# Earlier adjacency transposes, early TensorE work and later row sums in a two-layer graph network

## The chip, the cores and the metric

The kernel runs on one core of one Trainium2 chip. The metric is device time in microseconds for one launch, and lower is better. The core has five engines that run side by side, each working through its own list of instructions in order: TensorE (PE, matrix multiplication), VectorE (DVE), ScalarE (ACT), GpSimd (POOL) and SyncE (SP), which here issues nearly all transfers between device memory and on-chip memory. An engine waits only where an instruction names a semaphore that another engine or a transfer has yet to raise.

## What is computed

The input x has 16 batches of 1024 nodes with 256 channels; the adjacency is one 1024 x 1024 matrix for all batches. There are two layers, each closed by a layer norm without scale and offset. Cut to what matters:

```python
# layer 0, for each batch
c = mean(x over channels)                      # one number a node
A = 1 - |tanh((c_m - c_n) / 2)|                # likeness of two nodes, symmetric
g = relu((x.T @ (adj * A)) * para)             # the query graph: 256 x 1024
q = g as 4 heads of 64;  k, v = x @ kv_w       # keys and values
x = layernorm(x + softmax(q k.T / 8) v)
# layer 1
h = relu(x w1_loop + adj (x w1_neigh) + b1)    # 128 wide
h = relu(h w2_loop + adj (h w2_neigh) + b2)    # 256 wide
x = layernorm(x + (x + h) / 2)
```

Layer 0 needs the rows of adj as they lie (x.T times adj); layer 1 needs adj transposed. Everything is float32.

## The kernel before

**Stages.** The order of all work is written out by hand in `run()`; inside its `manual_schedule` block nothing is rearranged. For batch 0 the kernel makes keys (line 350) and values (362) from x, and then the query graph of batch 0: eight steps `q.step(t)` (line 400), each with one 128-row tile of the weighted adjacency `wg`. ScalarE makes the likeness (lines 386 and 387), VectorE multiplies it with adj (392). `q.end()` (lines 406 and 407) turns the sums into the queries qT. Then come 16 rounds, one a batch. Round b holds the attention of batch b in four units (`scores`: matmuls at 516, exponentials at 519, running sum of them on VectorE at 523 and 525; `outputs`: matmuls at 536), the first graph convolution of batch b-1 and the second of batch b-2 between the units, and after the last unit the query graph, keys and values of batch b+1. So each round ends in a transition, and it is there that the change works.

**Two kinds of query graph.** Batches 0 and 1 use `Queries`, with eight plain steps. Batches 2 to 15 use `FastQueries`, which builds the product from seven smaller products p[1] to p[7] in four steps (line 473). Its `end()` adds them up on VectorE: ScalarE copies p[1] to P1 (line 482), the first addition makes U (483), and five more lines (484 to 489) make the rest of U and qT. The seven products lie in PSUM: p[1] and p[6] in one tile of two banks, p[7] and p[5] in a second, p[2] and p[3] in a third, p[4] in a single bank. There are three such two-bank tiles in all, and the keys of the next batch take the first and then the second of them. The first half of the keys can therefore start when line 483 has read p[1] and p[6], and the second half when line 488 has read p[5].

**The norm.** The layer norm of layer 0 (`BlockedNorm`) runs during the same transition, on x in blocked form: `mean()` subtracts the mean of each row (lines 309 and 312, VectorE), `squares()` squares on ScalarE (318), sums the squares on VectorE (319) and joins the two halves (260), `variance()` folds the sums with a small matmul (256) between the two halves of the keys, `scale()` and `spread()` follow after the keys. For batches 1 to 14 `norm.mean()` and `norm.squares()` are called in the middle of the third step of the query graph, and `q.end()` comes one step later.

**The transposed adjacency.** It is made once. `adj_blocked(mt)` (line 207) loads 128 columns of adj with four transfers of 128 KB, in pieces of 128 bytes, so that a 32 x 32 transpose on VectorE (`turn_adj`, line 871) gives the full transpose: 16 instructions for eight tiles. Three quarters of the result stay in fixed tiles, the fourth in two tiles (rows01). In the kernel before, the loads are issued among the steps of the query graph of batch 1, and the 16 transposes come behind `norm.spread()` in the same transition. The first reader is the graph convolution of batch 0 in round 1 (line 654).

**Buffers and queues.** All 128 x 1024 working tiles come from one pool of 23 (`row_tile`). A transfer needs a free tile, and its completion is counted on one of eight counters in turn, so that SP holds a transfer back until the eighth one before it has landed. VectorE does what stands in its list in order: an instruction that waits for a transfer holds up everything behind it.

**The start.** x of batch 0 comes in four pieces (line 117). TensorE's first work is to transpose it (line 227), as each piece lands.

Of the kernel before, what the change touches and what calls it, by code (L numbers as in the profile page):

```python
# [12 lines left out]
AF = mybir.ActivationFunctionType  # L13
# [5 lines left out]
def kernel(  # L19
# [281 lines left out]
    class BlockedNorm:  # L301
# [10 lines left out]
                nc.vector.tensor_sub(x_cc, x_cc, mean.unsqueeze(2).to_broadcast([P, NB, S]))  # L312

        def squares(self):
            self.part = small.tile([P, NC, NB], F32, tag="part", name=f"sq_part_{self.name}", bufs=2)
            for cc in range(NC):
                sq = row_tile(f"sq_{self.name}_{cc}")
                nc.scalar.activation(sq, self.xB[cc], AF.Square)  # L318
                nc.vector.tensor_reduce(self.part[:, cc, :], by_node(sq), AX.X, ALU.add)  # L319
            join(self.part)  # L320

        def variance(self):
# [87 lines left out]
    class FastQueries(Queries):  # L410
# [61 lines left out]
                x_n, w_n = terms[n]  # L472
                nc.tensor.matmul(self.p[n], x_n[:, k, :], w_n, start=(k == 0), stop=(k == TJ - 1))  # L473

        def end(self):
            qT = work.tile([P, NC, N], F32, tag="qT", name=f"qT_{self.b}")
            u = row_tile(f"U_{self.b}")
            h0, h1 = ts(0, FB), ts(1, FB)
            p = self.p
            add = nc.vector.tensor_add  # L480
            p1 = row_tile(f"P1_{self.b}")[:, h0]
            nc.scalar.copy(p1, p[1])
            add(u[:, h0], p1, p[6])  # L483
            add(qT[:, 0, h0], p1, p[2])
            add(u[:, h1], u[:, h0], p[7])
            add(qT[:, 1, h0], u[:, h1], p[4])
            add(qT[:, 1, h1], u[:, h1], p[5])
            add(u[:, h0], u[:, h0], p[5])
            add(qT[:, 0, h1], u[:, h0], p[3])
            for cb in range(NC):  # L490
                nc.vector.tensor_mul(qT[:, cb, :], qT[:, cb, :], para_sb[:, cb, :])
                nc.scalar.activation(qT[:, cb, :], qT[:, cb, :], AF.Relu, scale=QSCALE)
            return qT
# [340 lines left out]
    def run():  # L834
# [3 lines left out]

        xT, c_col = prepare_first(x_first)
        q = Queries(0, x_first)
        for t in range(NT):
# [29 lines left out]
        for t in range(NT):  # L873
            if t + 3 < NT:
                q.weigh(t + 3)
            q.step(t)
            if t == 4:
                xB = load_blocked(0, "a0")
                ready = {}
                ready["xT"], ready["part"] = prepare(blocked, "1")  # L880
            if t == 6:
                ready["mean"] = means(ready["part"], "1")
        qT = q.end()
        convs = {}
        for b in range(B):
            more = b + 1 < B
            att = Attention(b, xB, qT, kT, v)
            c1, c2, c3 = (convs.get(b - k) for k in (1, 2, 3))
            both = Joined(c1, c2) if c2 else None
            if c1 and more:  # L890
                xb = load_x(b + 1, str(b + 1))
            if c2 and more:
                c2.load_h1()

            def gap0():
                blocked = load_blocked(b + 1, str(b + 1))
                c1.inner()
                att.add(0)
                if both:
                    c2.load_x()  # L900
                    both.fetch(2, 3)
                    both.left(nc.gpsimd)
                ready["xT"], ready["part"] = prepare(blocked, str(b + 1))

            def weigh_first():
                q.times_adj(0)
                q.times_adj(TJ)
                q.right(0)

            def next_means():  # L910
                q.c_row, q.c_col = means(ready["part"], str(b + 1))

            def gap1():
                for t in (0, TJ):
                    q.load(t)
                if both:
                    both.fetch(1, 4)
                    both.run({1: (lambda: q.left(nc.gpsimd),),
                              2: (lambda: att.add(1), next_means),
                              6: (lambda: q.likeness(0), lambda: c3 and c3.moments()),  # L920
                              7: (lambda: q.likeness(TJ),),
                              5: (weigh_first,),
                              4: (lambda: c3 and c3.finish(out[b - 3]),),
                              3: (c1.turn_blocks,)})
                else:
                    q.left(nc.gpsimd)
                    next_means()
                    att.add(1)
                    for t in (0, TJ):
                        q.likeness(t)  # L930
                    store("01", rows01)
                    adj_sums(rows01)
                    weigh_first()
                    c1.first(rows01)
                    c1.turn_blocks()

            def gap2():
                if both:
                    c2.last()
                att.add(2)  # L940

            between = [gap0, gap1, gap2] if c1 and more else []
            if more:
                q = (FastQueries if c1 else Queries)(b + 1, xb)
            for u in range(len(UNITS)):
                att.scores(u)
                if u == 3 and between:
                    for t in (2, TJ + 2, 3, TJ + 3):
                        q.load(t)
                    for t in (2, TJ + 2, 3, TJ + 3):  # L950
                        q.likeness(t)
                    q.right(1)
                if u and not between:
                    att.add(u - 1)
                att.outputs(u)
                if u == 2 and more:
                    if c1:
                        for t in (1, TJ + 1):
                            q.load(t)
                            q.likeness(t)  # L960
                            q.times_adj(t)
                    else:
                        q.c_row, q.c_col = ready["mean"]
                        for t in range(3):
                            q.load(t)
                            q.weigh(t)
                if u < 3 and between:
                    between[u]()
            norm = BlockedNorm(xB, att.sums, str(b))
            if more and not c1:  # L970
                xT = ready["xT"]
                for t in range(3, NT):
                    q.load(t)
                for t in range(3, NT):
                    q.likeness(t)
                for mt in range(4):
                    tiles[mt] = adj_blocked(mt)
                q.times_adj(3)
                q.step(0)
                q.times_adj(4)  # L980
                q.step(1)
                att.add(3)
                for mt in range(4, NT):
                    tiles[mt] = adj_blocked(mt)
                q.times_adj(5)
                q.step(2)
                q.step(3)
                norm.mean()
                q.times_adj(6)
                q.times_adj(7)  # L990
                q.step(4)
                norm.squares()
                q.step(5)
                q.step(6)
                norm.variance()
                xB = load_blocked(b + 1, f"a{b + 1}")
                q.step(7)
                qT = q.end()
                norm.scale()
                norm.spread()  # L1000
                turn_adj(range(NT))
                kT, v = keys(b + 1, xT), values(b + 1, xT)
            elif more:
                xT = ready["xT"]
                q.pair(2)
                q.step(0)
                q.step(1, lambda: att.add(3))
                q.pair(3)
                q.step(2, lambda: (norm.mean(), norm.squares()))
                q.step(3)  # L1010
                qT = q.end()
                xB = load_blocked(b + 1, f"a{b + 1}")
                kT = keys(b + 1, xT, norm.variance)
                norm.scale()
                norm.spread()
                v = values(b + 1, xT)
            else:
                c2.load_h1()
                c2.load_x()
                both.fetch(2, 3)  # L1020
                c1.inner()
                both.left(nc.gpsimd)
                both.fetch(1, 4)
                both.run({1: (lambda: att.add(3),), 2: (norm.mean, norm.squares), 7: (norm.variance,),
                          5: (norm.scale, norm.spread)})
                c1.turn(0)
                c2.last()
                c1.turn(1)
            convs[b] = GraphConv(b, norm.x1T, norm.nodes)
# [84 lines left out]
```

## Time and profile before

| | us |
|---|---|
| median of 3 runs | 2201.18 (2199.86 to 2201.87) |
| the profiled execution, its own time | 2200.6 |
| its span, first to last instruction | 2198.8 |
| TensorE busy | 2172.8 (99%) |
| VectorE busy | 1864.0 (85%) |
| ScalarE busy | 969.3 (44%) |
| mean granted TensorE clock | 0.997 |

The numbers in the first column of a timeline are microseconds from the start of the span. A group of instructions on one engine that follow each other is one row: its start, the time that it covers, engine, line, operation, the tiles written and read, shapes, and how many. In brackets stand the idle time of the engine just before and what ended it. PEld rows are weight loads of TensorE and run beside its matmuls. A float32 matmul of 512 columns is recorded as two passes, with starts 0.43 us apart when nothing is in the way. Ends of matmuls are modelled, so gaps are best read from starts. A line number is that of the kernel before; in the changed kernel lines from 318 on stand a few lines lower.

### The profile page before, as it was taken

How to read it: one execution, taken by the hardware profiler on the slowest of the kernel's cores; microseconds unless marked ns; L12 is line 12 of the kernel's file. 1: busy time of each engine (PE TensorE's matmuls, PEld its weight loads, DVE VectorE, ACT ScalarE, POOL GpSimd, SP SyncE). 2: the span in 40 equal slices, each digit the busy share in tenths (PEclk: the TensorE clock that was granted, in tenths of full speed). 3: DMA queues.
4: the chain of work that ended last, by engine and by line, in shares of the span. 5: the costliest groups of instructions: out<-in, count | busy, mean ns of one | idle time of the engine just before them, and what ended most of it. 6: DMA issues, size and time to landing. Idle time of an engine off the chain costs nothing.

```text
span 2198.8 us, 22720 instructions
## 1 busy us (share of the span) xinstructions
PE 2172.8 (99%) x8096; PEld 1032.4 (47%) x8096; DVE 1864.0 (85%) x2453; ACT 969.3 (44%) x1064; POOL 328.1 (15%) x177
## 2 busy tenths in 40 slices
PE   8998999999999999999999999999999999999997
PEld 4344444544444444444444445445454444544354
DVE  4988888888898988988889788998989889888965
ACT  4734445434454443545444454434544445434511
POOL 1000020210302103021030301203012020210021
PEclk9999999999999999999999999999999999999999
DMA  8294372633646335463453734527264272733342
GB/s 193 86 139 148 60 182 68 124 125 63 177 100 151 104 58 172 96 172 88 75 162 78 182 86 78 172 58 182 86 92 157 58 182 88 137 114 64 116 134 97
DMA packets 586359, 258.59 MB, mean 118 GB/s; under 512 B 488064, under 2 KB 552448, under 8 KB 586240
## 3 DMA queue, kind: packets, MB, share of 16 engines
q1 hardware_dynamic: 585968, 256.56, 48.4%
q8 instruction: 65, 1.06, 0.2%
q14 instruction: 54, 0.44, 0.1%
q10 hardware_dynamic: 272, 0.52, 0.1%
HBM read 210.90 MB, written 46.14 MB: 117 GB/s over the span
## 4 chain that ended last, share of the span: by engine, by line
PE 72%; DVE 24%; issue 2%; ACT 1%; DMA 0%; DVEq 0%; SPq 0%; POOLq 0%; ACTq 0%; POOL 0%
PE hu_ps L793 16%; PE s L516 15%; PE av L536 15%; DVE acc L525 6%; PE k_ps L350 5%; PE v_ps L362 5%; PE t_ps L634 3%; PE h_ps L700 2%; PE hu_ps L641 2%; PE g_ps L400 2%; PE h_ps L701 2%; DVE wg L392 2%; DVE sq_part L319 1%; DVE wg L446 1%; DVE T L445 1%
## 5 line engine op out<-in xcount | busy, mean ns | idle before, releaser
L519 ACT ACTIVATE pr<-s 128x1024 f32<-128x1024 f32 x512 | 476.1, 1052 | 179.5 <-PE s L516 179.1
L525 DVE TENSOR_TENSOR acc<-acc,pr 128x1024 f32<-128x1024 f32 x384 | 493.2, 1285 | 41.4 <-DVE acc L525 0.9
L516 PE MATMUL s<-qT,kT 64*128 64x512 f32 x2048 | 457.2, 596 | 0.7 <-ACT qT L407 0.7
L536 PE MATMUL av<-pr,v 128*64 128x512 f32 x2048 | 453.6, 595 | 0.0
L516 PEld LDWEIGHTS s<-qT,kT 64*128 64x128 f32 x2048 | 190.9, 186 | 236.5 <-ACT pr L519 114.8
L536 PEld LDWEIGHTS av<-pr,v 128*64 128x64 f32 x2048 | 141.4, 137 | 300.0 <-issue 289.7
L326 POOL TENSOR_TENSOR rstd<-rstd,neg_half 128x32 f32<-128x32 f32 x16 | 87.1, 5441 | 1149.9 <-DVE rstd L324 1149.9
L386 ACT ACTIVATE wg<-c_row,c_col 128x1024 f32<-128x1024 f32 x128 | 147.1, 1149 | 86.5 <-DVE accB L527 50.6
L392 DVE SCALAR_TENSOR_TENSOR wg<-wg,adj 128x1024 f32<-128x1024 f32 x128 | 149.9, 1211 | 10.4 <-ACT wg L387 10.4
L793 PE MATMUL hu_ps<-adj,R 128*128 128x512 f32 x360 | 158.3, 596 | 0.0
L387 ACT ACTIVATE wg<-wg 128x1024 f32<-128x1024 f32 x128 | 135.4, 1058 | 4.1
L350 PE MATMUL k_ps<-xT,kvw_sb 128*128 128x512 f32 x256 | 117.9, 605 | 2.9 <-DVE U L483 2.8
L318 ACT ACTIVATE sq<-xB_a 128x1024 f32<-128x1024 f32 x32 | 33.8, 1057 | 192.4 <-DVE xB_a L312 178.8
L473 PE MATMUL g_ps<-wg,S 128*128 128x512 f32 x224 | 116.7, 603 | 0.0
L473 PE MATMUL g_ps<-T,S 128*128 128x512 f32 x224 | 114.4, 592 | 0.0
L362 PE MATMUL v_ps<-kvw_sb,xT 128*128 128x256 f32 x512 | 113.1, 379 | 0.0
L331 DVE TENSOR_TENSOR xB_a<-xB_a,rstd 128x1024 f32<-128x1024 f32 x32 | 38.8, 1255 | 84.4 <-POOL rstd L326 84.4
L473 PE MATMUL g_ps<-wg,x 128*128 128x512 f32 x224 | 109.0, 599 | 0.0
L362 PEld LDWEIGHTS v_ps<-kvw_sb,xT 128*128 128x128 f32 x512 | 97.3, 190 | 20.1 <-issue 7.7
L523 DVE TENSOR_TENSOR acc<-pr,pr 128x1024 f32<-128x1024 f32 x64 | 78.1, 1220 | 33.8 <-ACT pr L519 33.8
L793 PE MATMUL hu_ps<-adjT,t 128*128 128x512 f32 x240 | 105.7, 592 | 0.0
L793 PEld LDWEIGHTS hu_ps<-adj,R 128*128 128x128 f32 x360 | 67.3, 190 | 78.9 <-issue 75.8
(167 smaller groups left out, 2718.7 us busy)
## 6 DMA issues: line engine op xcount, KB each, us to landing
adj<-in_adj_dram SPq DMA_DIRECT2D x128, 512.0 KB, 4.5
adj<-adjT SPq DMA_DIRECT2D x120, 512.0 KB, 7.5
xB_a<-in_x_dram SPq DMA_DIRECT2D x128, 128.0 KB, 4.1
x1d<-xB_a SPq DMA_DIRECT2D x128, 128.0 KB, 3.4
x<-x1d SPq DMA_DIRECT2D x16, 1024.0 KB, 6.8
xB<-in_x_dram SPq DMA_DIRECT2D x120, 128.0 KB, 4.6
x<-in_x_dram SPq DMA_DIRECT2D x15, 1024.0 KB, 7.0
out_dram<-x SPq DMA_DIRECT2D x15, 1024.0 KB, 4.6
```

Source lines behind the costliest of these rows:

```text
L326: nc.gpsimd.tensor_tensor(self.rstd, self.rstd, neg_half, ALU.pow)
L350: nc.tensor.matmul(pk[:, ts(j, FB)], kvw_sb[:, cc, ts(kb, P)], xT[:, cc, ts(j, FB)], start=(cc == 0), stop=(cc == NC - 1))
L362: nc.tensor.matmul(pv[:, ts(i, C)], xT[:, cc, ts(g * per + i, P)], kvw_sb[:, cc, C:2 * C], start=(cc == 0), stop=(cc == NC - 1))
L386: nc.scalar.activation(wg, self.c_row, AF.Abs, bias=self.c_col[:, t:t + 1], scale=-1.0)
L387: nc.scalar.activation(wg, wg, AF.Tanh, scale=-0.5)
L392: nc.vector.scalar_tensor_tensor(wg, wg, 1.0, self.adj.pop(t), op0=ALU.add, op1=ALU.mult)
L473: nc.tensor.matmul(self.p[n], x_n[:, k, :], w_n, start=(k == 0), stop=(k == TJ - 1))
L516: nc.tensor.matmul(ps[:, ts(s, FB)], self.kT[rows, pair, ts(mt, P)], self.qT[rows, pair, ts(j, FB)], start=True, stop=True)
L519: nc.scalar.activation(pr, ps, AF.Exp)
L525: nc.vector.tensor_add(acc, acc, pr)
L536: nc.tensor.matmul(pav[s * HD:(s + 1) * HD, :], self.v[:, mt, pair * P + s * HD:pair * P + (s + 1) * HD], self.pr[mt][:, ts(s, FB)], start ...
L793: nc.tensor.matmul(dst, self.x[n][:, k, :], half_adj[w][:, k, :] if w else of_rows(rows, k), start=(start and k == 0), stop=(k == TJ - 1), ...
```

## The change

There are three parts.

1. Sixteen transposes of the identity into an unused PSUM bank are put ahead of all other work of TensorE.
2. The eight loads of columns of adj are issued in the query graph of batch 0: tiles 0 to 3 after step 2, tiles 4 to 7 after step 4, the latter ahead of the load of x for the residual of batch 0 (xB). The transposes of tiles 0 to 4 stand behind `prepare` of batch 1 in VectorE's list, ahead of `means` and `q.end()`; those of tiles 5 to 7 stand behind `q.end()`. The old places are empty.
3. `squares()` is cut in two: it keeps the squares on ScalarE, and the new `sum_squares()` has the sums on VectorE. In batches 1 to 14 (14 transitions) the sums are handed to `q.end()`, which calls them just behind its first addition. In batches 0 and 15 both parts are called one after the other, as before.

```diff
         def squares(self):
+            self.sq = [row_tile(f"sq_{self.name}_{cc}") for cc in range(NC)]
+            for cc in range(NC):
+                nc.scalar.activation(self.sq[cc], self.xB[cc], AF.Square)
+
+        def sum_squares(self):
             self.part = small.tile([P, NC, NB], F32, tag="part", name=f"sq_part_{self.name}", bufs=2)
             for cc in range(NC):
-                sq = row_tile(f"sq_{self.name}_{cc}")
-                nc.scalar.activation(sq, self.xB[cc], AF.Square)
-                nc.vector.tensor_reduce(self.part[:, cc, :], by_node(sq), AX.X, ALU.add)
+                nc.vector.tensor_reduce(self.part[:, cc, :], by_node(self.sq[cc]), AX.X, ALU.add)
             join(self.part)
...
-        def end(self):
+        def end(self, between):
...
             add(u[:, h0], p1, p[6])
+            between()
             add(qT[:, 0, h0], p1, p[2])
...
+        idle = bank_psum("idle")
+        for _ in range(16):
+            nc.tensor.transpose(idle[:, 0:P], ident, ident)
         xT, c_col = prepare_first(x_first)
...
             q.step(t)
+            if t in (2, 4):
+                for mt in range(2 * t - 4, 2 * t):
+                    tiles[mt] = adj_blocked(mt)
             if t == 4:
                 xB = load_blocked(0, "a0")
                 ready = {}
                 ready["xT"], ready["part"] = prepare(blocked, "1")
+                turn_adj(range(5))
             if t == 6:
                 ready["mean"] = means(ready["part"], "1")
         qT = q.end()
+        turn_adj(range(5, NT))
...
-                for mt in range(4):
-                    tiles[mt] = adj_blocked(mt)
...
-                for mt in range(4, NT):
-                    tiles[mt] = adj_blocked(mt)
...
-                turn_adj(range(NT))
                 kT, v = keys(b + 1, xT), values(b + 1, xT)
...
                 q.step(2, lambda: (norm.mean(), norm.squares()))
                 q.step(3)
-                qT = q.end()
+                qT = q.end(norm.sum_squares)
```

More of the change, by code (lines that the diff above doesn't have):

```diff
@@ L992, in run @@
                 norm.squares()
+                norm.sum_squares()
                 q.step(5)
@@ L1023, in run @@
                 both.fetch(1, 4)
-                both.run({1: (lambda: att.add(3),), 2: (norm.mean, norm.squares), 7: (norm.variance,),
+                both.run({1: (lambda: att.add(3),), 2: (norm.mean, norm.squares, norm.sum_squares), 7: (norm.variance,),
                           5: (norm.scale, norm.spread)})
```

## The prediction

> **What bounds the kernel now.** I read first the list of TensorE's own waits: engine and line, what ended the wait, microseconds in total, how often, the longest.
>
> ```profile
> PE den_ps L548 <- DVE o L540: 5.6, 1, 5.6
> PE xT_ps L227 <- DMA x<-in_x_dram: 4.9, 2, 4.7
> PE k_ps L350 <- DVE U L483: 2.8, 13, 0.5
> PE den_ps L548 <- DVE den_part L529: 0.8, 1, 0.8
> PE s L516 <- ACT qT L407: 0.7, 1, 0.7
> ```
>
> With one more row of 0.7 this is all: 15.5 us of 2198.8. TensorE is the bound nearly everywhere, so the most that a change outside TensorE can win is some 15 us, while any new wait of TensorE costs its full length. The three parts of the change aim at three of these rows: the second (start), the first (one gap of round 1) and the third (14 transitions).
>
> Next the timeline of one transition, of 14 that look alike:
>
> ```profile
> 393.15 2.36 DVE L312 TENSOR_TENSOR xB_a<-xB_a,mean 128x1024 f32<-128x1024 f32 x2
> 395.56 2.35 DVE L319 TENSOR_REDUCE sq_part<-sq 128x32 f32<-128x1024 f32 x2
> 396.57 0.57 ACT L482 COPY P<-g_ps 128x512 f32<-128x512 f32 x1
> 398.06 0.68 DVE L483 TENSOR_TENSOR U<-P,g_ps 128x512 f32<-128x512 f32 x1
> 398.79 3.70 PE L350 MATMUL k_ps<-xT,kvw_sb 128*128 128x512 f32 x8 [0.17 <-DVE U L483]
> 401.18 0.68 DVE L488 TENSOR_TENSOR U<-U,g_ps 128x512 f32<-128x512 f32 x1
> 402.33 0.30 PE L256 MATMUL sum_ps<-sq_part,fold 128*128 128x32 f32 x2
> 402.47 1.96 PE L350 MATMUL k_ps<-xT,kvw_sb 128*128 128x512 f32 x4
> ```
>
> The sums (L319) stand ahead of U, and the keys' first half starts when U ends. The second half (402.47) needs L488 done; that ended at 401.86, so here it is hidden by 0.6 us.
>
> Then the end of the query graph of batch 0:
>
> ```profile
> 39.02 0.19 DVE L260 TENSOR_TENSOR part<-part 128x32 f32<-128x32 f32 x1
> 48.32 0.19 DVE L265 TENSOR_SCALAR mean<-mean_ps 128x32 f32<-128x32 f32 x1 [9.11 <-PE mean_ps L256]
> 50.12 1.23 DVE L406 TENSOR_TENSOR qT<-g_ps,para_sb 128x1024 f32<-128x1024 f32 x1
> 56.01 1.22 DVE L523 TENSOR_TENSOR acc<-pr,pr 128x1024 f32<-128x1024 f32 x1 [2.95 <-ACT pr L519]
> ```
>
> VectorE is idle for 9.1 us and again for 3.0 us: this is the room into which the transposes are moved. TensorE's scores start at 52.49, on L406 and the ScalarE step behind it. Last, the transposes' old place and what follows:
>
> ```profile
> 145.45 9.57 DVE L871 STREAM_TRANSPOSE adjT<-adjB 128x512 f32<-128x512 f32 x16
> 155.37 1.22 DVE L523 TENSOR_TENSOR acc<-pr,pr 128x1024 f32<-128x1024 f32 x1 [0.36 <-ACT pr L519]
> 170.33 0.52 DVE L552 RECIPROCAL rden<-den_ps 64x16 f32<-64x16 f32 x2 [2.60 <-PE den_ps L548]
> 190.28 0.64 PE L548 MATMUL den_ps<-den_part,fold 128*128 128x32 f32 x2 [5.56 <-DVE o L540]
> ```
>
> and the rate of the loads (issues by SP; then a window with its GB/s at the end):
>
> ```profile
> 115.55 22.81 SPq L207 DMA_DIRECT2D adjB<-in_adj_dram  x25
> 116.00:138.00 22.00, 22.00 (x57) 10.03 (x56) 17.35 (x25) 2.11 (x2) 2.61 (x1) 1.00 1.31 144
> ```
>
> 25 loads of 128 KB in 22.81 us, 144 GB/s: 0.91 us each.
>
> **What the Trainium skill says.** The page "TensorE: Matmul & The Clock Gate", section "HAM oscillation — how this bites in real kernels", says that an idle TensorE of over about 3.4 us falls to half clock. The trace agrees: behind the 5.6 us gap at 190.28 the window from 190 to 192 us shows a clock of 0.50, and the four matmul passes there are 0.86 us apart instead of 0.43. The same page's Part 4 says that transposes don't count as work in this; here 16 transposes from 4.73 us are followed by key passes that still start 0.86 us apart, which fits but doesn't prove it. "DMA: Bandwidth & Descriptors", section "Why small descriptors are slow (HBM only)", gives a fixed cost per descriptor; the 144 GB/s with 128-byte pieces against 325 GB/s in the window from 10 to 24 us agree in kind.
>
> **The change part by part.** *Transposes leave their old place.* 9.57 us of VectorE go. What is late next? L523 at 155.37 starts on ScalarE's exponential, after 0.36 us of idle, so it can't start earlier; and VectorE is idle again for 2.60 us at 170.33, waiting for TensorE. So no debt of the transposes reaches the gap at 190.28: that debt begins at 170.33, with four 1.2 us instructions of prepare (L216, L249) between. Gain 0 (bounds 0 to 8.7: the 5.6 gap, 2.0 of half clock behind it, 0.8 of the next wait). The loads that leave SP's queue there free it for loads that were on time: 0.
>
> *Loads in the new place.* The first eight take the slots in which xB's eight went before: issued from 28.50, the last at 39.1, landed 3.8 later, at 42.9. Transfers 9 to 20 (through tile 4) follow at 0.91: 42.9 + 12 x 0.91 = 53.8; tile 7 lands at 42.9 + 24 x 0.91 = 64.7. Bounds for the spacing: 0.64 (206 GB/s, window 29 to 36 us, with long rows in it) to 1.17 (112 GB/s, 37 to 43 us). xB is now behind all 32 and lands at 64.7 + 8 x 0.91 = 72.0; its first reader is the first `att.add` at 83.1: hidden by 11 us. Behind it on SP stands the first row tile of batch 1, issued at 66.96 before, needed at 100.1: hidden. The three tiles beyond the 23 take places of adj rows long used: 0.
>
> *Transposes in the new place.* 0.60 us each (9.57/16). Those of tile 4 wait for 53.8, and VectorE's list is held: behind them stand L265, c_row, and L406, on which the scores wait. They end at 53.8 + 1.2 = 55.0. L265 to L406 is 1.80 (50.12 - 48.32), L406 to scores 2.37 (52.49 - 50.12): scores start at 59.2 instead of 52.49, +6.7 (bounds 3.5 to 9.8). TensorE has then been idle for some 8 us, so it starts at half clock: +2.0, as behind 190.28 (four passes at +0.43, and 0.3 around them; bounds 1 to 3.4). The last three tiles end at 64.7 + 1.2 = 65.9; L523 would be due at 56.01 + 6.7 + 2.0 = 64.7. It is 1.2 late, and before the second unit VectorE idles for 1.63 us (at 69.99, on ScalarE): hidden. Without that cover 1.2. Sum of this part: +8.7.
>
> *Transposes of the identity.* 16 x 0.22 us from 1.5 to 5.0 us, 0.3 beyond the first piece of x. If they warm the clock, the half-clock passes (0.7 us) and part of the slow transposes of x go, up to 1.2 us by 12.7 us. But the scores at 59.2 hang on transfers, so this shows as longer idle: 0 (bounds -1.2 to +0.3).
>
> *Sums behind U.* U now needs only the copy P, ended at 397.14, and L312, ended at 395.51: it starts at 397.2, 0.86 earlier, and ends at 397.9. The last graph pass started at 398.03, so the keys start at 398.46, not 398.79: -0.33. The sums then take VectorE for 2.50 us (395.56 to 398.06). The next addition starts at 397.2 + 0.60 + 2.50 = 400.3 instead of 398.66: +1.64. With it L488 ends at 403.5. In the built program the keys' second half waits for just this instruction. TensorE would be there at 398.46 + 3.68 = 402.14 (3.68 from 402.47 - 398.79); it waits 1.4 us and starts at 403.55 instead of 402.47: +1.08. Behind it stand the values and the next scores, with no idle time of TensorE until the next transition, so nothing gives it back. On ScalarE the copies of keys and values come up to 1.64 later; the third group of values needs the first copy at 275.8 in the first transition, and it is there at about 275.5: hidden by 0.3. 14 x 1.08 = +15.1 (bounds 0.9 to 1.3 each: 12.6 to 18.2).
>
> Sum: 2200.6 + 8.7 + 15.1 = 2224.4 for the profiled execution; its time is 0.6 under the median, so 2201.2 + 23.8 = 2225.0.
>
> **The rivals.** *The first graph is free* (B). If tile 4 were there by 48.3, VectorE's idle 9.1 us would hide the ten transposes. That needs 0.45 us a load, half of what the trace shows anywhere for such pieces. Then +15.1 - 1.2: 2215.1.
>
> *The keys' second half doesn't wait* (C). If its tile came free earlier than I read, each transition wins its 0.33: 2201.2 + 8.7 - 14 x 0.33 = 2205.3. Against it: the wait on L488 stands in the program before too.
>
> *VectorE sets the period* (D, not slower). The chain of waits goes through VectorE for 24%, and the steps ahead of U in each transition are its own. If TensorE's even starts hid waiting, a delay of TensorE would be taken up before the next transition, and U's 0.86 would be won: 2201.2 - 14 x 0.86 + 8.7 = 2197.9. The point that decides: TensorE would need over 1.08 us of slack in each round; the list shows 2.8 us in the whole run, at U itself.
>
> **How the numbers follow.** Forecast 0.80, B 0.08, C 0.05, D 0.05, something slower still 0.02. The forecast's bounds are +17 to +31: 2218 to 2232. Reaching to B gives 2213 to 2232. A measurement can tell some 0.2% (4.4 us) from no change: faster 0.02 (D's tail), same 0.06 (half of C, most of D), slower 0.92.
>
> **What would show it.** In the profile after: a wait of TensorE at the keys for the line of L488, 14 times, 1.4 us each; the wait for U gone; the wait of 5.6 us at L548 still there; a VectorE wait for adjB of some 3 us and more ahead of tile 4's transposes; scores of batch 0 at about 59 us with a clock of 0.5. I am wrong if the second half starts within 3.7 us of the first, if the scores start by 53, or if the gap near 190 is gone.

## The result, and the profile after

The changed kernel takes 2228.03 us, the median of 4 runs (2226.10 to 2231.87), against 2201.31 for the kernel before in the same session: 1.0125 times, interval 1.0107 to 1.0142. That is 26.7 us more; the prediction had 23.8 (2225.0, range 2213 to 2232). The profiled execution took 2228.1 us with a span of 2226.2, 27.4 longer than before.

First the list of TensorE's own waits in the changed kernel (engine and line, what ended the wait, us in total, how often, the longest):

```profile
PE k_ps L353 <- DVE U L492: 18.4, 14, 1.6
PE s L520 <- ACT qT L410: 10.0, 1, 10.0
PE den_ps L552 <- DVE o L544: 5.6, 1, 5.6
PE den_ps L552 <- DVE den_part L533: 2.1, 3, 0.8
PE mean_ps L256 <- DVE o L544: 0.9, 4, 0.2
```

L492 is the addition that was L488 before. The wait for U is gone, and 14 waits for L492 of 1.3 us each stand in its place. The start of the scores of batch 0 now costs one wait of 10.0 us. The wait of 5.6 us in round 1, which the earlier transposes were to help, is unchanged. The fourth row has grown from 0.8 and the fifth is new; the prediction had neither. (A row of 1.5 us between them, ahead of the transposes of the identity, is left out here.)

The timeline of the transition that the prediction showed, now in the changed kernel:

```profile
407.23 0.57 ACT L485 COPY P<-g_ps 128x512 f32<-128x512 f32 x1
407.83 0.69 DVE L486 TENSOR_TENSOR U<-P,g_ps 128x512 f32<-128x512 f32 x1 [1.66 <-ACT P L485]
408.44 2.34 DVE L322 TENSOR_REDUCE sq_part<-sq 128x32 f32<-128x1024 f32 x2
409.14 3.60 PE L353 MATMUL k_ps<-xT,kvw_sb 128*128 128x512 f32 x8
413.43 0.68 DVE L492 TENSOR_TENSOR U<-U,g_ps 128x512 f32<-128x512 f32 x1
414.17 3.70 PE L353 MATMUL k_ps<-xT,kvw_sb 128*128 128x512 f32 x8 [1.29 <-DVE U L492]
```

VectorE now idles 1.66 us ahead of U, because the sums no longer fill that time. Then the sums run between U and the rest of the additions. The second half of the keys starts 5.03 us after the first (414.17 - 409.14) instead of 3.68.

And the end of the first query graph, TensorE and VectorE:

```profile
46.87 3.68 PE L403 MATMUL g_ps<-wg,x 128*128 128x512 f32 x8
48.08 1.30 DVE L879 STREAM_TRANSPOSE adjT<-adjB 128x512 f32<-128x512 f32 x2 [2.21 <-DMA adjB<-in_adj_dram]
51.80 1.30 DVE L879 STREAM_TRANSPOSE adjT<-adjB 128x512 f32<-128x512 f32 x2 [2.41 <-DMA adjB<-in_adj_dram]
55.32 1.30 DVE L879 STREAM_TRANSPOSE adjT<-adjB 128x512 f32<-128x512 f32 x2 [2.22 <-DMA adjB<-in_adj_dram]
56.55 0.15 DVE L265 TENSOR_SCALAR mean<-mean_ps 128x32 f32<-128x32 f32 x1
```

VectorE waits more than 2 us for each tile of columns and can take the mean only at 56.55 instead of 48.32; the scores start at 60.55, with a clock of 0.50 in the window from 60 to 62 us.

**Where the 27.4 us came from.** I took the starts of the first key matmul of each batch from both traces. In the first of the 14 transitions the changed kernel is 9.35 us late (273.42 against 264.07): this is the first graph. From the first to the last transition it loses another 16.89 (1769.24 against 1752.35 us). One regular round takes 135.76 us instead of 134.72, so 13 rounds give 13.5, and 3.4 are left for single rounds that take up to 1.3 more. In the last transition the second half of the keys adds 1.35. The end gives back 0.2. The kernel before has a few such rounds too (135.07 us at most), so the 3.4 are what the changed kernel has beyond them.

### The profile page after: what moved, and what is told of

Its sections match the earlier page's. It is cut to its first block, busy times and chain, and to the rows that moved or that the text cites. A ratio compares the mean times of both kernels' runs of the same rounds, so it can differ in the third digit from the quotient of the medians.

```text
span 2226.2 us, 22744 instructions
## 1 busy us (share of the span) xinstructions
PE 2176.2 (98%) x8112; PEld 1038.9 (47%) x8112; DVE 1865.6 (84%) x2453; ACT 968.4 (43%) x1064; POOL 327.9 (15%) x177
## 4 chain that ended last, share of the span: by engine, by line
PE 52%; DVE 34%; SPq 6%; issue 3%; ACT 2%; DMA 2%; POOL 1%; DVEq 0%; ACTq 0%; POOLq 0%
PE hu_ps L797 15%; PE s L520 11%; PE av L540 10%; DVE acc L529 9%; PE v_ps L365 3%; SPq L108 3%; DVE wg L395 3%; PE h_ps L704 2%; PE h_ps L705 2%; PE hu_ps L645 2%; PE k_ps L353 2%; PE t_ps L638 2%; DVE accB L531 1%; DVE sq_part L322 1%; SPq L207 1%
```

## The theories

- **Mine, from the prediction**: the first graph waits for transfers, through VectorE; and the keys' second half waits for an addition that the sums hold up. To it I added after the result: the later rstd (the inverse deviation of the norm) holds up the stores of x1d on SP, and behind them the loads of the next batch's x, so that VectorE is late in some rounds.
- **Rivals**: the three parts collide, and their costs are not separate; the keys wait for something other than VectorE's time; the old place of the transposes was worth something that other parts of the change hid; the late x is chance.

## Each part alone

Each of these three kernels is the one before with one part of the change.

**p1_warm**, the 16 transposes of the identity:

```diff
+        idle = bank_psum("idle")
+        for _ in range(16):
+            nc.tensor.transpose(idle[:, 0:P], ident, ident)
         xT, c_col = prepare_first(x_first)
```

> Only the 16 transposes of the identity are added to the kernel before. My theory: keys, values and first graph of batch 0 end some 1.2 us earlier (in the changed kernel TensorE reached its last graph passes at 46.87 instead of 48.12), and with nothing later in the way scores of batch 0 start up to 1.2 us before 52.49: 2200.0 to 2201.3, a gain too small for a verdict but visible in the trace. Rival: the scores hang on VectorE's steps (mean, c_row, qT), which hang on transfers, so that the scores start at 52.4 to 52.5 as before and the time is 2201.3.

Measured: 2200.69 us, 0.9996 times (0.9988 to 1.0005). The scores of batch 0 start at 51.46 instead of 52.49. The full clock is granted at 4.80 us instead of 9.99. One pair of profiles does not give the size of this, for both numbers differ from profile to profile. In the nine kernels here without this part and without the move of all eight tiles, the kernel before among them, the full clock comes at 8.46 to 10.63 us and the scores start at 51.77 to 52.84; in p1_warm and best, the two that have this part and adj in its old place, it comes at 4.80 and 7.58 and they start at 51.46 and 51.28. So the scores do move, which puts the rival out, by 0.3 to 1.6 us; the time cannot be told from no change.

**p2_adj**, the loads and transposes of adj moved as in the change:

> Only the loads and transposes of adj are moved into the first graph. My theory: VectorE waits for the loads of tiles 0 to 4 ahead of the mean, scores start at 60.0 to 60.6 instead of 52.49, TensorE then runs four passes at half clock (2 us), the wait of 5.6 us near 190 stays: 2201.3 + 9.6 = 2211 (2209 to 2212). Rival: with TensorE not warmed ahead, the old place gives something back that the other parts hid (the wait of 5.6 us gets shorter): 2203 to 2206.

Measured: 2211.91 us, 1.0045 times (1.0029 to 1.0062), +10.5. The scores start at 59.97, and the wait near 200 (190 before) is 5.56 us as ever. The rival is out.

**p3_sums**, the sums behind U:

> Only the sums of squares stand behind U in 14 transitions. My theory: the keys' second half waits 1.3 us for L488 each time, net 1.04 with U's own 0.33 won, and the x of the next batch comes later, so that some rounds lose another 1.2 us: 14 x 1.04 + 3.4 = +18, 2219 (2215 to 2221). Rival: the extra 1.2 us in some rounds of the changed kernel come from the shift by the first graph and not from the sums; then only 14 x 1.04 = +14.6, 2215.9, and no wait of VectorE for x of the next batch.

Measured: 2216.16 us, 1.0067 times (1.0050 to 1.0084), +14.7. The waits for L492 are 18.9 us in 14, and a regular round takes 135.77. The median lies at the rival's value, but the rival's other half fails: VectorE waits for the next batch's x 5 times, 3.1 us in all. So such waits do not need the shift by the first graph. The three parts alone sum to -0.8 + 10.5 + 14.7 = 24.4 of the 26.7; what is left is within the intervals. The parts don't collide in any large way.

## Is it VectorE's time between U and L492?

**p3_twice** takes each sum twice:

```diff
-            for cc in range(NC):
+            for cc in (0, 1, 0, 1):
                 nc.vector.tensor_reduce(self.part[:, cc, :], by_node(self.sq[cc]), AX.X, ALU.add)
```

> As the sums alone, but each sum is taken twice, so that 2.34 us more of VectorE lie between U and the addition that frees the bank of the keys' second half. My theory: the wait grows by just that, to 3.6 us each, 14 x 2.34 = 33 us more than with the sums once: 2251 to 2253; [...]TensorE may fall to half clock behind it, which would give 2 us more each (up to 2280). Rival: the keys' second half waits for something else (the copy of the keys' first half on ScalarE, or the release of another bank), and the time grows by less than half of 33 us.

Measured: 2268.71 us, 1.0311 times (1.0293 to 1.0328). TensorE's timeline in one transition:

```profile
545.07 0.41 PE L256 MATMUL sum_ps<-sq_part,fold 128*128 128x32 f32 x2 [0.59 <-DVE sq_part L260]
548.18 5.40 PE L353 MATMUL k_ps<-xT,kvw_sb 128*128 128x512 f32 x8 [2.70 <-DVE U L492]
```

The fold of the sums now waits as well, so the wait comes in two parts, 0.59 and 2.70 us. In most of the 14 transitions (11 in the clock's record) a window of 3.41 us at half clock follows, which is why the eight passes here take 5.40 us instead of 3.70. The one round that is free of it and of a late x takes 138.03 us, most others some 139.7: 1.7 us is what the half clock costs, and 138.03 - 135.77 = 2.26 is what two more sums of 1.17 cost. The wait grows with VectorE's time, one for one; the rival is out.

**p3_small** leaves the sums out: a copy of 32 elements of each tile of squares stands in their place, so the norm divides by other numbers.

```diff
-                nc.vector.tensor_reduce(self.part[:, cc, :], by_node(self.sq[cc]), AX.X, ALU.add)
+                nc.vector.tensor_copy(self.part[:, cc, :], self.sq[cc][:, 0:NB])
```

> As the sums alone behind U, but the sums over nodes of the squares are left out: a copy of 32 elements of each tile of squares stands in their place (0.1 to 0.2 us), so that the deviations are of other numbers. My theory: no wait of TensorE for L488, and U earlier, so each transition wins its 0.33 us: 2201.3 - 4.6 = 2196.7 (2196 to 2199, with some late x of the next batch). Rival (the place behind U, with squares on ScalarE beside the copy P, costs by itself): 2201 or more.

Measured: 2195.24 us, 0.9974 times (0.9962 to 0.9985). No wait is left at either half of the keys, and a regular round takes 134.28 us, 0.44 less than before. The place behind U costs nothing by itself. The time is 0.8 us under my range: beside the 0.33 us of U, each transition wins 0.11, because the keys' second half starts 3.57 us behind the first instead of 3.68.

**p3_half** leaves the first sum ahead of U, where VectorE waits for the copy P anyway, and puts the second behind it.

```diff
         def squares(self):
...
+            self.sum_squares(0)
...
             add(u[:, h0], p1, p[6])
+            between()
```

> As the sums alone, but only the second of the two sums stands behind U; the first stays ahead of it (where VectorE waits for the copy P anyway). U is 0.86 earlier than before, the addition L488 then comes 1.25 - 0.86 = 0.4 later than before, where it had 0.6 us of room. My theory: U's wait is gone and no wait, or one of 0.1, takes its place at the keys' second half; rstd and the x loads stay where they were: 2201.3 - 14 x 0.25 = 2197.8 (2196.5 to 2199.5). Rival (any reduction behind U costs, since VectorE is the bound through the transition): a wait of 0.5 us and more at the keys' second half, 2203 and more.

Measured: 2201.58 us, 1.0001 times (0.9992 to 1.0009). U is earlier and its wait gone, but L493 (before's L488) is waited for in its place: 2.8 us in all over 13, the very figure that U had before. A regular round takes 134.64 us. My forecast of 2197.8 failed: L488 had 0.55 us of room before (0.61, less 0.06 from an awaited end to the start). It now ends 0.45 later behind the last graph pass, which I had seen, and the keys themselves come 0.33 earlier since U no longer holds them, which I had not: 0.55 - 0.45 - 0.33 = -0.23, and they wait. The 0.1 a round that were left went into waits for a late x (3.4 us in 7). The rival's waits of 0.5 us and more are not the rule either: the wait is 0.2 on average and 0.5 at most.

Put in a row by the number of sums of 1.17 us behind U, a regular round takes 134.28, 134.64, 135.77 and 138.03 us with none, one, two and four; before it was 134.72 with both ahead of U. The first sum is nearly hidden, each further one costs its full length.

## The first graph: transfers or transposes?

**p2_two** moves only tiles 0 and 1, loads and transposes; the other six keep the old place.

```diff
+            if t == 2:
+                for mt in range(2):
+                    tiles[mt] = adj_blocked(mt)
...
+                turn_adj(range(2))
...
-                turn_adj(range(NT))
+                turn_adj(range(2, NT))
```

> As the adj move alone, but only tiles 0 and 1 are moved into the first graph; tiles 2 to 7 keep their old place. These two land by 39.8 and 43.3 where all eight are moved, before VectorE's next step is due at 48.3. My theory (VectorE is held by the loads of tiles 2 to 4, not by the transposes themselves, and the old place is worth nothing): scores of batch 0 start at 52.5 with the clock at 1.0, the wait of 5.6 us near 190 stays: 2201.3 (2200.5 to 2202.5). Rival 1 (the additional transfers slow the rows of adj for the first graph): TensorE waits in the first graph, 2203 and more. Rival 2 (the old place is worth something): the wait near 190 gets shorter by up to 2.4 us, 2199.

Measured: 2201.12 us, 1.0000 times (0.9991 to 1.0009). The timeline of this kernel:

```profile
43.65 1.30 DVE L871 STREAM_TRANSPOSE adjT<-adjB 128x512 f32<-128x512 f32 x2 [2.43 <-DMA adjB<-in_adj_dram]
48.65 0.19 DVE L265 TENSOR_SCALAR mean<-mean_ps 128x32 f32<-128x32 f32 x1 [3.70 <-PE mean_ps L256]
52.82 1.56 PE L516 MATMUL s<-qT,kT 64*128 64x512 f32 x6 [0.69 <-ACT qT L407]
```

Tile 1 has landed and is turned 3.70 us before the mean is due, and the scores start 4.37 us behind the last eight graph passes (48.45), as before (52.49 - 48.12 = 4.37). So four transposes in VectorE's idle time are free, and taking 2.4 us of VectorE out of the old place wins nothing: the wait in round 1 is still 5.6. What costs in the change is what stands behind them, the waiting for tiles 2 to 4.

**gapD** asks why the old place was worth nothing. In round 1 the first denominator's matmul is put ahead of the graph's t_ps:

```diff
-                c1.inner()
+                if both:
+                    c1.inner()
                 att.add(0)
+                if not both:
+                    c1.inner()
```

> The kernel before with one edit in round 1: the first denominator's matmul stands ahead of the graph's t_ps instead of behind it. It tests why the transposes' leaving gave nothing. My theory: VectorE sets round 1 from 170.33 on, where it waits 2.60 us for this matmul; with that wait gone the 5.6 us of TensorE near 190 shrink to 2 to 3, and [...]the half clock behind them goes too: -2.5 - 2.0 = 2196.8 (2196 to 2199). Rival (VectorE is held by the x of batch 2 or by the exponentials, and its debt comes back at the next denominator near 224): 2200 to 2201.3, or the 0.8 us there grow by what is won.

Measured: 2201.00 us, 0.9998 times (0.9989 to 1.0007). VectorE's wait of 2.60 us is gone, and TensorE's wait shrinks from 5.56 to 3.81 us, with one window of half clock of 3.41 us instead of 6.83. Most of the window that is gone lay in the wait, though: from the start of the matmul that waited to the second pass of the graph convolution behind it (line 654), 4.17 us go by instead of 4.45, so only 0.3 is saved. TensorE now waits 0.78 us for the first denominator itself, and VectorE loses most of what it won:

```profile
167.47 1.27 POOL L434 TENSOR_TENSOR S<-x 128x512 f32<-128x512 f32 x1
167.66 1.63 DVE L556 TENSOR_TENSOR o<-o,rden 128x512 f32<-128x512 f32 x1
168.69 1.72 POOL L435 TENSOR_TENSOR S<-x,S 128x512 f32<-128x512 f32 x1
169.32 1.64 DVE L558 TENSOR_TENSOR xB_a<-xB_a,o 128x512 f32<-128x512 f32 x1
```

L556 and L558 took 0.69 us each in the kernel before, where GpSimd's four additions had ended at 170.68 and these two began at 171.09. Here they lie beside GpSimd and take 1.63 and 1.64: 1.9 of the 2.6 us are lost again. So it holds that VectorE's list from 170.33 on sets the wait in round 1, but my price for the edit, 4.5 us, did not come. The median lies at the rival's value, though its growing wait near 224 is not there (0.78 us in both). By that point TensorE is 1.82 us ahead of the kernel before (222.96 against 224.78), and 0.7 of this stems from the start (scores at 51.77 against 52.49); one later round with a late x, 135.81 us against 134.99, gives 0.8 back.

## The late x of the next batch

The changed kernel's late rounds look like this one (VectorE and TensorE):

```profile
584.88 1.25 DVE L216 STREAM_TRANSPOSE xT<-xB 128x1024 f32<-128x1024 f32 x1 [1.33 <-DMA xB<-in_x_dram]
602.03 0.41 PE L552 MATMUL den_ps<-den_part,fold 128*128 128x32 f32 x2 [0.65 <-DVE den_part L533]
```

VectorE waits 1.33 us for the second half of the next batch's x; 17 us later TensorE waits for the denominator that VectorE makes. That round takes 137.07 us. The loads of this x stand on SP behind the eight stores of x1d, which wait for rstd. In the transition of the timelines above, the first store is issued 13.09 us behind the first key matmul before (411.88 - 398.79), and 14.99 behind it in the changed kernel (424.13 - 409.14).

**p3_end** puts the norm later still: the sums stand behind the whole end of the query graph, and their fold behind the first group of values.

```diff
                 qT = q.end()
+                norm.sum_squares()
                 xB = load_blocked(b + 1, f"a{b + 1}")
-                kT = keys(b + 1, xT, norm.variance)
+                kT = keys(b + 1, xT)
+                v = values(b + 1, xT, between=norm.variance)
                 norm.scale()
                 norm.spread()
-                v = values(b + 1, xT)
```

> The sums stand behind the whole query graph's end (behind L491) instead of behind U, and the matmul that folds them behind the first group of values. My theory: U is as early as in the changed kernel (-0.33 each), the wait for L488 is gone. But rstd comes 2.8 us later than before, and with it the stores of x1d on SP, and the loads of the next batch's x queued behind them: VectorE waits for these in every round, 1.5 to 2.8 us, and TensorE then for den_part: 2201.3 - 4.6 + 14 x 1 to 2.5 = 2211 to 2232. Rival (the late x seen in the changed kernel is chance and not the queue): no more than a few us of such waits, 2197 to 2201.

Measured: 2241.73 us, 1.0173 times (1.0144 to 1.0201). From the list of all waits of this kernel:

```profile
DVE xT L216 <- DMA xB<-in_x_dram: 23.4, 14, 3.0
PE den_ps L553 <- DVE den_part L534: 17.0, 14, 2.9
```

The wait for L488's successor is gone, and the late x comes in every round. It is dearer than I forecast, for two reasons that the trace shows: small waits around the fold of the sums (6.4 us in all), and a window of half clock of 3.41 us behind four of the waits, 1.7 us each if they cost what they did in p3_twice. The four runs do not agree: three took 2240.6 to 2243.1 us with a mean clock of 0.993 and one 2230.85 with 0.996, so that this part comes and goes.

**p3_end_stores** is the same with the stores of x1d issued behind those loads:

```diff
             def gap0():
                 blocked = load_blocked(b + 1, str(b + 1))
+                ready.pop("write", lambda: None)()
...
-                norm.spread()
+                norm.spread(b + 2 == B)
+                if b + 2 < B:
+                    ready["write"] = norm.write
```

> As with the sums behind the query graph's end, but the eight stores of x1d are issued behind the eight loads of the next batch's x instead of ahead. My theory: the loads are no longer behind rstd on SP, VectorE's wait for them is gone, and U's gain shows: 2196 to 2199. Rival (the loads wait for something else, or the stores, later now, hold the load of x1d for the graph of two batches before): VectorE or TensorE waits elsewhere, 2205 and more.

Measured: 2208.59 us, 1.0033 times (1.0021 to 1.0046). VectorE waits for no x, and the late rounds are gone: 33 us by one edit of SP's order, or 22 against the fastest run of p3_end. The rest of my forecast failed. A regular round takes 135.32 us, not 134.28:

```profile
406.58 1.89 PE L371 MATMUL v_ps<-kvw_sb,xT 128*128 128x256 f32 x8
408.64 0.41 PE L256 MATMUL sum_ps<-sq_part,fold 128*128 128x32 f32 x2 [0.17 <-DVE sq_part L260]
409.33 1.99 PE L371 MATMUL v_ps<-kvw_sb,xT 128*128 128x256 f32 x8 [0.28 <-DVE rstd L327]
```

The fold waits for the sums and the second group of values for rstd, which must first read the result of the fold. Between the first group's start and the second's lie 2.75 us, where eight passes at 0.215 and a fold of 0.14 would need 1.86: 0.9 of the 1.04.

**after_stores** puts the same edit of the stores into the changed kernel.

> The changed kernel with the eight stores of x1d issued behind the loads of the next batch's x. My theory (VectorE's waits for that x come from the queue: rstd, then the stores, then the loads): they go, and with them the 1.2 us that some rounds lose beyond the regular 135.76; the wait for L488 stays: 2228.0 - 3.4 = 2224.6 (2223.5 to 2226). Rival (chance of the memory): 2227 to 2229, with such waits left.

Measured: 2224.94 us, 1.0108 times (1.0091 to 1.0125), 3.1 under the changed kernel. By the intervals alone the two could be equal. In the trace VectorE's waits for the next batch's x are gone, and 11 of the 13 periods between the transitions lie within 0.1 us of 135.76 (the others 136.00 and 136.11). With p3_end and p3_end_stores this shows that the order on SP decides whether x is late. How much of the changed kernel's lateness is due to the sums is not shown: p1_warm (1.2 us in 2 waits) and p2_adj (2.1 in 4) have such waits with the sums in their old place, and p3_small, which leaves the sums out, has 3.6 in 4, as much as the changed kernel (3.5 in 5); the kernel before has none. The loads land within a microsecond or so of when they are needed, so that small shifts show. What tips a single round is open.

## A version faster than both

**best** is the kernel before with the identity transposes, the stores behind the loads, one sum ahead of U, and the other behind the additions that free the second bank of the keys, which come first now:

```diff
-            for n in (1, 6, 2, 7, 4, 5, 3) if k == TJ - 1 else (1, 2, 3, 5, 7, 6, 4):
+            for n in (1, 6, 7, 5, 2, 4, 3) if k == TJ - 1 else (1, 2, 3, 5, 7, 6, 4):
...
             add(u[:, h0], p1, p[6])
-            add(qT[:, 0, h0], p1, p[2])
             add(u[:, h1], u[:, h0], p[7])
-            add(qT[:, 1, h0], u[:, h1], p[4])
             add(qT[:, 1, h1], u[:, h1], p[5])
             add(u[:, h0], u[:, h0], p[5])
+            between()
+            add(qT[:, 0, h0], p1, p[2])
+            add(qT[:, 1, h0], u[:, h1], p[4])
             add(qT[:, 0, h1], u[:, h0], p[3])
```

> The kernel before with four edits: the transposes of the identity; one of the two sums behind the additions, one ahead of U; the stores of x1d behind the loads of the next batch's x; and in the query graph's end the three additions that read the terms 7 and 5 right behind U, ahead of the sum (with the last pass of TensorE in the order 1, 6, 7, 5, 2, 4, 3), so that the bank of the keys' second half is free before VectorE takes the sum. The adjacency keeps its old place. My theory: neither U nor the keys' second half is waited for, and no late x: the period falls from 134.72 to 134.28, 14 x 0.44 = 6.2, and 0.8 at the start: 2201.3 - 7 = 2194.3 (2193.5 to 2196.5). Rival (the order of additions moves the wait to the fold of the sums, or to qT and the scores behind it): a wait of 0.3 us and more in each transition, 2199 and more.

Measured: 2194.78 us, 0.9970 times the kernel before (0.9959 to 0.9982), 6.8 us less. The timeline of a transition:

```profile
397.97 3.60 PE L358 MATMUL k_ps<-xT,kvw_sb 128*128 128x512 f32 x8
398.80 0.68 DVE L494 TENSOR_TENSOR U<-U,g_ps 128x512 f32<-128x512 f32 x1
399.39 1.21 DVE L322 TENSOR_REDUCE sq_part<-sq 128x32 f32<-128x1024 f32 x1
401.40 0.30 PE L256 MATMUL sum_ps<-sq_part,fold 128*128 128x32 f32 x2
```

The last reader of p[5], L494, ends at 399.48, two microseconds before the keys' second half is due at 401.55; the sum comes behind it and is still in time for its fold. No wait at the keys is left in the list, and no wait for x. A regular round takes 134.34 us, and the rounds of up to 135.07 us that the kernel before has are gone too. The profiled span is 4.8 us shorter: 0.4 by the first transition, 5.9 between the first and the last (13 x 0.38 = 4.9 of it by the regular round), 1.5 given back behind the last, which stays open.

## Why the prediction was right, step by step

- **Transposes leave their old place, gain 0**: right. The wait of 5.6 us stands in the changed kernel, in p2_adj and in p2_two.
- **Loads in the new place**: the spacing was right. Tiles are turned 3.62 us apart from the first to the fifth (40.84 to 55.32), 0.905 us a load; forecast 0.91. The landing of tile 4 was put at 53.8 and it is turned at 55.32: the start of the row of loads was set some 1.5 us too early. The wait of 3 us and more ahead of tile 4 came as 2.2 to 2.9 us ahead of each of the first five tiles.
- **Scores and the cold clock**: forecast 59.2, measured 60.55, for that 1.5. The half clock cost 1.6 us over the first four passes (0.58, 0.42, 0.42 and 0.20 beyond the usual 0.43), forecast 2.0; in p2_adj it lasted seven passes and cost 3.0. The part came to 9.4 at the first transition and 10.5 alone, forecast 8.7, inside its bounds.
- **Transposes of the identity, 0 within the change**: right. TensorE starts the last pass of the first graph 2.0 us earlier than in p2_adj (49.96 against 51.91), and this goes into the wait for qT, 10.0 us instead of 7.5.
- **Sums behind U, +1.08 a round**: 1.04 measured (135.76 - 134.72), the wait 1.3 against 1.4. The wait for U vanished as said.
- **Rivals**: C fell with the 14 waits, D with the period that rose by nearly the whole delay, B with the wait for qT.
- **What was missing**: the step said that "Behind it stand the values and the next scores, with no idle time of TensorE until the next transition" and left out the queue on SP, where the next x stands behind the stores of x1d. With the stores behind the loads most of the 3.4 us of late rounds go, and after_stores takes 2224.94 us where the forecast was 2225.0. That the later sums brought these rounds about is not shown, as p3_small loses as much. The agreement is also in part chance: the first graph came out higher than forecast, by 0.7 us in the changed kernel and 1.8 alone, and the sums alone lower, 14.7 against 15.1; by the single parts, the first graph would make up most of the 2.9 us by which the forecast was short. The intervals are too wide to tell which it is.

## What to carry to other kernels

When an engine that fills its waiting time with other work is given that work later, look at everything behind it in its list up to the last instruction that frees a buffer someone waits for, and put those first: with both sums between U and that instruction a round took 1.04 us longer, while in best one of them stands behind it and nothing waits. A step moved later takes along what hangs on it, and a queue that works in order passes the delay on to loads that have nothing to do with it, as p3_end shows. Transfers into an idle stretch of an engine are free only as far as they land before that engine's next due instruction.

## What the runs showed of the hardware that I had not expected

- Transposes warm the clock. In the four kernels with 16 of the identity from 1.53 us on, the full clock is granted at 4.80 (p1_warm), 5.64 (the changed kernel), 6.98 and 7.58 us, each time when TensorE had done nothing but transposes, for its first key pass starts at 7.96 or later. In the ten others its first work is the transposes of x from 4.65 us or later, and the full clock comes at 8.46 to 11.31. The Trainium skill, "TensorE: Matmul & The Clock Gate", Part 4, says that transposes do not count as busy in the same way and that the full clock does not engage for them; these runs say otherwise, and the measurement decides (the trace records these transposes as plain MATMUL, so whether they run in the mode that the page means is open).
- The same page's Part 1 has the clock released after about 3.4 us of sustained activity. Here it came 3.3, 4.1, 5.5 and 6.1 us after the first transpose, so 3.4 us is about the least.
- The clock also falls behind waits shorter than the 3.4 us of that page's section "HAM oscillation — how this bites in real kernels": behind 0.59 and 2.70 us with one small matmul between (p3_twice), and in p3_end behind waits of 1.58 us (at 1010 us) and 1.23 us (at 1563 us), each with one of 0.21 after it. Other waits of that size were spared. All windows of half clock in the middle of the runs last 3.41 us or a multiple of it.
- Additions on VectorE of 128 x 512 took 1.63 us beside additions on GpSimd and 0.69 without (gapD against before). What the two engines contend for, no run here tries.
